# Joining the last two layers of a four-layer graph network in one loop

## The chip, the cores and the metric

The kernel runs on one core of one Trainium2 chip. The metric is device time in microseconds (us) of one execution of the whole kernel. Before the change it is 2429.77 us, the median of 3 runs from 2427.74 to 2431.06.

The core's engines are named as in the profile: PE is TensorE (matmuls; PEld is its weight load), DVE is VectorE, ACT is ScalarE, POOL is GpSimd, SP is SyncE, which here only issues transfers. SPq and ACTq are the queues in which SP and ScalarE issue DMAs.

## The reference

A graph of 4096 nodes with 128 features each, X (4096 x 128), goes through four layers. Each layer adds its output to X and normalises every row: X = layernorm(X + layer(X, adj)). adj is a symmetric 0/1 matrix of 4096 x 4096 with ones on the diagonal. The layers are, by the numbers used in the code:

- layer 0: a hyperbolic graph convolution with sigmoid attention
- layer 1: a graph transformer with four heads
- layer 2: relu((D (adj + I) D X) W2), with D the diagonal matrix of (row sum + 1)^-0.5
- layer 3: attention with H = X W3^T + b, s = H a_s, r = H a_r, weights softmax over j, where adj is 1, of leaky_relu(s_i + r_j), and output att H

In layer 3 the softmax is computed factored. With adj of zeros and ones, exp(leaky_relu(s + r)) is exp of the larger of (s + r) and 0.2 (s + r). Divided by a factor that depends on i alone, it becomes max(exp(0.8 s_i), exp(-0.8 r_j)) exp(r_j). So one vector `rho` = exp(0.8 s), laid along the free axis, one column `col[:, 0]` = exp(-0.8 r) and features F = X exp(r) are enough: the inner loop takes one maximum and one product with adj for each element.

## The kernel before, in words

X stays in on-chip memory for the whole kernel, as 32 tiles of 128 rows. Layer 0 writes a transposed copy of adj to memory (`adjT`), cut into 8 x 8 blocks of 512 x 512 (1 MB each in float32); layers 1, 2 and 3 read it block by block. I counts output blocks of 512 nodes (four tiles of X), J the blocks that are summed over. All matmuls are in float32 and appear in the profile as two records each.

**End of layer 0.** For each of the 32 tiles, L494 adds the layer's output to X. After every fourth, `normalise_tile` (L164) is called: statistics of the four tiles on DVE (L146, L147), variance plus epsilon (L170), Sqrt on ScalarE (L171), a reciprocal on DVE (L172), and then the normalisation. Here it is called with `on_scalar=True`: DVE makes `ms` = -mean / std (L175) and ScalarE applies it (L181). Layer 1 then begins with transposes of X (L112) and, for each block of 512 columns, products pk and pq (L825, L836), whose results ScalarE and DVE split and stack.

**Layer 2** (`layer2`, L1179). With `d` = (deg + 1)^-0.5 (L1191 to L1193), Y = X d. For each I, PE sums Y^T over the eight blocks into `pa` (L1200 adds the identity, L1212 the blocks, four matmuls of 128 x 512 each). The blocks are fetched into eight buffers `at` (L1210), even J from ScalarE's queue, odd J from SP's. DVE checks each block for values other than 0 and 1 (`odd`, L1222). After the eighth block ScalarE copies `pa` (L1227), PE multiplies with W2 into `pb` (L1230), DVE scales and clips (L1234), adds to X (L1236), and `normalise_tile(I)` follows, on DVE at L185.

**Layer 3** (`layer3`, L1240). It starts when layer 2 has ended. Small matrices are prepared from W3 and the attention vectors: `us`, `ur`, `cb`, `wx` (L1259 to L1285). X is transposed as a whole (L1289), `pr` (L1292) gives r for each tile, `psr` (L1299) gives s along the free axis, DVE adds the bias to give `rho` (L1300) and takes maxima of the absolute values (L1301). The column sums of X (`pm`, L1307) go to `tot`. A maximum over all of these and over `odd` is compared with LIMIT; all engines read the flag `fi` (L1321) and branch: `attend_factored` if the values are small and adj is plain, else `attend`, a general version that this input does not take.

`attend_factored` (L1327) first makes the exps (L1335 to L1339), F = X exp(r) (L1341, L1342) and X + bias (L1344), and then loops over I and J. A block is fetched into six buffers (L1350). For each of its four slices, DVE makes w = max(rho, col) x adj (L1354, four buffers) and PE multiplies it with F into `pa` (L1357). After the last block ScalarE copies `pa`, PE multiplies with `wx` into `pb` (L1367), DVE divides and adds to X (L1372), `normalise_tile(I)` follows and the rows go out (L1376).

**What sets the order.** Apart from the loop of layer 1, no order is written by hand: a scheduler places each engine's instructions by dependences and its own estimates, so an instruction can stand earlier or later on its engine than in the source. Every engine, and each queue that issues DMAs, works through its instructions in that order. ScalarE's activation functions come in table sets; where a function of a set that is not loaded stands next, the build puts a table load (ACT_TABLE_LOAD) before it.

Of the kernel before, what the change touches and what calls it, by code (L numbers as in the profile page):

```python
# [9 lines left out]
F32 = mybir.dt.float32  # L10
# [6 lines left out]
P = 128  # L17
# [13 lines left out]
class Net:  # L31
# [132 lines left out]
    def normalise_tile(self, I, on_scalar=False):  # L164
# [6 lines left out]
        nc.scalar.activation(rs, rs, AF.Sqrt)  # L171
        nc.vector.reciprocal(rs, rs)  # L172
# [1006 lines left out]
    def layer2(self, weight):  # L1179
        nc, tc, N, NT, NS, D, X = self.nc, self.tc, self.N, self.NT, self.NS, self.D, self.X  # L1180
        with ExitStack() as ctx:
            keep = ctx.enter_context(tc.tile_pool(name="keep2", bufs=1))
            rot = ctx.enter_context(tc.tile_pool(name="rot2", bufs=2))
            at2 = ctx.enter_context(tc.tile_pool(name="at2", bufs=8))
            ps_a = ctx.enter_context(tc.tile_pool(name="ps_a", bufs=2, space=PSUM))
            ps_b = ctx.enter_context(tc.tile_pool(name="ps_b", bufs=2, space=PSUM))
            Y = keep.tile([P, NT, D], F32, tag="Y", name="Y")
            w = self.load_mat(weight, "w2")

            d = self.deg  # L1190
            nc.vector.tensor_scalar(d, d, 1.0, 1e-8, op0=ALU.add, op1=ALU.add)  # L1191
            nc.scalar.activation(d, d, AF.Sqrt)
            nc.vector.reciprocal(d, d)  # L1193
            for t in range(NT):
                nc.vector.tensor_scalar(Y[:, t, :], X[:, t, :], d[:, t : t + 1], None, op0=ALU.mult)
            for I in range(NS):

                pa = ps_a.tile([P, S], F32, tag="pa", name="pa")
                for b in range(4):
                    nc.tensor.matmul(  # L1200
                        pa[:, b * P : (b + 1) * P],
                        lhsT=Y[:, 4 * I + b, :],
                        rhs=self.ident,
                        start=(b == 0),
                        stop=False,
                        skip_group_check=True,
                    )
                for J in range(NS):
                    at = at2.tile([P, 4, S], F32, tag="at", name="at")
# [19 lines left out]
                for b in range(4):  # L1229
                    nc.tensor.matmul(pb[:, b, :], lhsT=a[:, b * P : (b + 1) * P], rhs=w, start=True, stop=True)  # L1230
# [251 lines left out]
```

## Time and profile before

| what | value |
|---|---|
| median of the runs | 2429.77 us (2427.74 to 2431.06, 3 runs) |
| the profiled execution | 2428.91 us, span 2427.1 us |
| busy share of the span: PE, DVE, ACT, POOL | 84%, 79%, 61%, 3% |
| mean granted clock of PE | 0.919 |
| chain that ended last: PE, DVE, ACT, issue, DMA | 58%, 24%, 12%, 3%, 2% |
| L1357, matmuls of layer 3: 512, two records each | 9% of the chain on the page |
| L1212, matmuls of layer 2: 512 records | 223.1 us busy, no idle time before them |

The profile is of one execution. Its times count from the start of the span. Each line of a timeline has start, length, engine, line, operation, tile written <- tiles read, shapes, how many were merged, and in brackets how long the engine was idle before and what it waited for. "x2 records" of a float32 matmul are one instruction. Layer 0 ends near 977 us, layer 2 begins near 1884, layer 3 near 2130. The shares are averages over stages with different limits, so the stages concerned are read one by one.

### The profile page before, as it was taken

How to read it: one execution, taken by the hardware profiler on the slowest of the kernel's cores; microseconds unless marked ns; L12 is line 12 of the kernel's file. 1: busy time of each engine (PE TensorE's matmuls, PEld its weight loads, DVE VectorE, ACT ScalarE, POOL GpSimd, SP SyncE). 2: the span in 40 equal slices, each digit the busy share in tenths (PEclk: the TensorE clock that was granted, in tenths of full speed). 3: DMA queues.
4: the chain of work that ended last, by engine and by line, in shares of the span. 5: the costliest groups of instructions: out<-in, count | busy, mean ns of one | idle time of the engine just before them, and what ended most of it. 6: DMA issues, size and time to landing. Idle time of an engine off the chain costs nothing.

```text
span 2427.1 us, 24381 instructions
## 1 busy us (share of the span) xinstructions
PE 2048.1 (84%) x8923; PEld 1138.3 (47%) x8923; DVE 1910.2 (79%) x2726; ACT 1486.0 (61%) x1793; POOL 69.5 (3%) x87
## 2 busy tenths in 40 slices
PE   4477887787777771889999999999998899979998
PEld 4266666566666650634333333433333344444443
DVE  6478888788778888767877878777787887668887
ACT  5688889888888877478777787878776000010000
POOL 2000000000000051100000000000000000000000
PEclk7689989899888885999999999999999899979999
DMA  2455466555555630154454444545444788528774
GB/s 52 139 185 200 143 207 210 172 181 183 186 169 173 195 105 1 61 200 171 154 182 153 168 173 154 176 158 179 158 160 162 279 287 284 206 104 298 286 286 170
DMA packets 103768, 431.44 MB, mean 178 GB/s; under 512 B 8976, under 2 KB 19280, under 8 KB 62672
## 3 DMA queue, kind: packets, MB, share of 16 engines
q1 hardware_dynamic: 85200, 295.50, 35.9%
q10 hardware_dynamic: 18432, 134.23, 15.9%
q8 instruction: 74, 1.21, 0.2%
q14 instruction: 62, 0.51, 0.1%
HBM read 356.26 MB, written 73.43 MB: 177 GB/s over the span
## 4 chain that ended last, share of the span: by engine, by line
PE 58%; DVE 24%; ACT 12%; issue 3%; DMA 2%; SPq 0%; ACTq 0%; POOL 0%; DVEq 0%; POOLq 0%
PE pv L965 15%; PE pa L1357 9%; PE pa L1212 9%; PE ps L939 9%; DVE e L948 5%; PE pz L583 4%; DVE w L606 3%; PE pi L674 3%; DVE w L636 3%; DVE t L632 3%; PE ptA L564 3%; ACT t L628 3%; ACT e L946 2%; ACT at L572 2%; ACT w L601 1%
## 5 line engine op out<-in xcount | busy, mean ns | idle before, releaser
L948 DVE SCALAR_TENSOR_TENSOR e<-at,e 128x2048 f32<-128x2048 f32 x256 | 581.6, 2287 | 181.0 <-ACT e L946 171.3
L946 ACT ACTIVATE e<-ps 128x1024 f32<-128x1024 f32 x512 | 489.4, 1025 | 130.6 <-PE ps L939 101.8
L965 PE MATMUL pv<-e,VA 128*64 128x512 f32 x2048 | 503.5, 613 | 12.2 <-DVE e L948 12.2
L939 PE MATMUL ps<-QS,KS 128*128 128x512 f32 x1024 | 313.1, 425 | 27.7 <-ACT e L946 23.3
L939 PEld LDWEIGHTS ps<-QS,KS 128*128 128x128 f32 x1024 | 173.3, 190 | 246.0 <-ACT e L946 153.6
L674 PE MATMUL pi<-HA,w 128*128 128x129 f32 x1152 | 186.7, 337 | 83.2 <-DVE w L636 83.2
L965 PEld LDWEIGHTS pv<-e,VA 128*64 128x64 f32 x2048 | 126.0, 137 | 258.1 <-issue 232.2
L1357 PE MATMUL pa<-w,F 128*128 128x512 f32 x512 | 223.2, 597 | 12.2 <-DVE w L1354 12.2
L674 PEld LDWEIGHTS pi<-HA,w 128*128 128x128 f32 x1152 | 179.8, 249 | 93.8 <-DVE w L636 93.8
L1212 PE MATMUL pa<-at,Y 128*128 128x512 f32 x512 | 223.1, 596 | 0.0
L1354 DVE SCALAR_TENSOR_TENSOR w<-rho,col,at 128x512 f32<-128x512 f32 x256 | 186.7, 746 | 18.9 <-PE pa L1357 1.7
L591 DVE SCALAR_TENSOR_TENSOR t<-ei,de,pz 128x512 f32<-128x512 f32 x144 | 107.2, 747 | 106.5 <-PE pz L583 102.7
L564 PE MATMUL ptA<-ident,ad 128*128 128x128 f32 x1032 | 146.0, 287 | 42.9 <-ACT at L572 35.7
L1222 DVE SCALAR_TENSOR_TENSOR odd<-at 128x2048 f32<-128x2048 f32 x64 | 146.6, 2290 | 38.3 <-DMA at<-adjT 37.6
L564 PEld LDWEIGHTS ptA<-ident,ad 128*128 128x128 f32 x1032 | 124.9, 148 | 99.4 <-ACT at L572 53.3
L572 ACT COPY at<-ptA 128x512 f32<-128x512 f32 x200 | 108.3, 587 | 99.0 <-PE ptA L564 98.8
L583 PE MATMUL pz<-HT 128*128 128x512 f32 x292 | 161.6, 664 | 4.9 <-DVE w L655 4.5
L1357 PEld LDWEIGHTS pa<-w,F 128*128 128x128 f32 x512 | 97.3, 192 | 133.9 <-issue 100.1
L1212 PEld LDWEIGHTS pa<-at,Y 128*128 128x128 f32 x512 | 97.5, 192 | 120.0 <-issue 118.8
L606 DVE TENSOR_TENSOR w<-w,at 128x2048 f32<-128x2048 f32 x64 | 143.7, 2281 | 0.0
L1361 ACT COPY a<-pa 128x512 f32<-128x512 f32 x8 | 4.7, 586 | 206.1 <-PE pa L1357 206.1
L931 ACT ACTIVATE nat<-nat 128x2048 f32<-128x2048 f32 x64 | 122.7, 1918 | 1.9 <-DMA nat<-in_adj_dram 1.9
(351 smaller groups left out, 2448.8 us busy)
## 6 DMA issues: line engine op xcount, KB each, us to landing
at<-adjT SPq DMA_DIRECT2D x128, 1024.0 KB, 4.8
ad<-in_adj_dram SPq DMA_DIRECT2D x64, 1024.0 KB, 6.5
adjT<-at SPq DMA_DIRECT2D x64, 1024.0 KB, 8.3
nat<-in_adj_dram ACTq DMA_DIRECT2D x64, 1024.0 KB, 4.9
at<-adjT ACTq DMA_DIRECT2D x64, 1024.0 KB, 4.8
dj<-rows SPq DMA_DIRECT2D x28, 256.0 KB, 7.6
X<-in_x_dram SPq DMA_DIRECT2D x4, 512.0 KB, 6.5
di<-rows SPq DMA_DIRECT2D x8, 256.0 KB, 8.4
```

Of the source, the lines that this page charges most:

```text
L564: nc.tensor.transpose(pt[:, ib, :], st[p]["ad"][k][:, ib, jb * P : (jb + 1) * P], self.ident)
L572: copy(st[p]["at"][k][:, jb, :], st[p]["pt"].pop(m))
L583: nc.tensor.matmul(pz, lhsT=HT[:, j * P : (j + 1) * P], rhs=HT[:, I * S : (I + 1) * S], start=True, stop=True)
L606: nc.vector.tensor_tensor(w, w, at, ALU.mult)
L674: nc.tensor.matmul(self.po[ib // 2][:, ib % 2, :], lhsT=w[0][:, jb, ib * P : (ib + 1) * P], rhs=HA[:, 4 * J + jb, :], start=False, stop=(J ...
L939: nc.tensor.matmul(p[:, h, :], lhsT=KS[:, h2 + h, jb * P : (jb + 1) * P], rhs=QS[I % 2][:, h2 + h, :], start=True, stop=True,)
L946: nc.scalar.activation(e[:, h2 : h2 + 2, :], p, AF.Exp)
L948: nc.vector.scalar_tensor_tensor(e, at[:, jb % 4, :].unsqueeze(1).to_broadcast([P, NH, S]), 0.0, e, op0=ALU.not_equal, op1=ALU.mult,)
L965: nc.tensor.matmul(st["po"][h // 2][g : g + 64, :], lhsT=VA[:, o : o + 64], rhs=e[:, h, :], start=(jb == 0), stop=(jb == NT - 1), skip_gro ...
L1212: nc.tensor.matmul(pa, lhsT=Y[:, 4 * J + jb, :], rhs=at[:, jb, :], start=False, stop=(J == NS - 1 and jb == 3), skip_group_check=True,)
L1354: nc.vector.scalar_tensor_tensor(w, rho[:, I * S : (I + 1) * S], col[:, 0, j : j + 1], at[:, jb, :], op0=ALU.max, op1=ALU.mult)
L1357: nc.tensor.matmul(pa, lhsT=F[:, j, :], rhs=w, start=False, stop=(j == NT - 1), skip_group_check=True)
```

## The change

- `normalise_tile` makes 1/std with two ScalarE activations, Ln and then Exp with scale -0.5, where it had Sqrt on ScalarE and a reciprocal on DVE. It is called at the end of layer 0 and for every I of layers 2 and 3.
- `layer2` and `layer3` become one function, `layers23`. The small matrices of layer 3 are made before layer 2's loop. The rest of layer 3's preparation becomes `prepare(I)`, called after `normalise_tile(I)`: transposes of the four tiles, `pr`, `psr`, bias and clamping of r and s to 40 in size, maxima, the three exps, F, and X + bias, which has a buffer of its own, `XB`.
- The column sums of X come from ScalarE's copy of the transposed tiles (an accumulated sum, `part`), and one transpose at the end, in place of the `pm` matmuls.
- The `at` buffers of layer 2 become six instead of eight. Three buffers `ahead` hold the blocks (0, 0) to (0, 2) for layer 3; their fetches are written after the flag and before the branch, and `attend_factored` reads them instead of fetching these blocks again.
- `attend`, the general version, takes over buffers and is no longer pipelined.

```diff
@@ normalise_tile
-        nc.scalar.activation(rs, rs, AF.Sqrt)
-        nc.vector.reciprocal(rs, rs)
+        nc.scalar.activation(rs, rs, AF.Ln)
+        nc.scalar.activation(rs, rs, AF.Exp, scale=-0.5)
@@ layers23 (was layer2, layer3)
+            ahead = [keep.tile([P, 4, S], F32, tag=f"ahead{J}", name=f"ahead{J}") for J in range(3)]
             F = keep.tile([P, NT, D], F32, tag="F", name="F")
+            XB = keep.tile([P, NT, D], F32, tag="XB", name="XB")
...
-            at2 = ctx.enter_context(tc.tile_pool(name="at2", bufs=8))
+                atp = pctx.enter_context(tc.tile_pool(name="at2", bufs=6))
...
+                def prepare(I):
+
+                    s, tl = slice(I * S, (I + 1) * S), slice(4 * I, 4 * I + 4)
+                    p = self.ps_t.tile([P, 4, P], F32, tag="pt", name="pt")
+                    for b in range(4):
+                        nc.tensor.transpose(p[:, b, :], X[:, 4 * I + b, :], self.ident)
+                    XT = rot.tile([P, S], F32, tag="XT", name="XT")
+                    nc.scalar.activation(
+                        XT, p.rearrange("p a b -> p (a b)"), AF.Identity, accum_out=part[:, I : I + 1]
+                    )
+                    pr = ps_s.tile([P, S], F32, tag="ps", name="pr")
+                    for b in range(4):
+                        nc.tensor.matmul(
+                            pr[:, b : b + 1], lhsT=XT[:, b * P : (b + 1) * P], rhs=ur, start=True, stop=True
+                        )
+                    ps = ps_s.tile([P, S], F32, tag="ps", name="psr")
+                    nc.tensor.matmul(ps, lhsT=us, rhs=XT, start=True, stop=True)
+                    r = rot.tile([P, 4], F32, tag="r", name="r")
+
+                    nc.vector.tensor_scalar(r, pr[:, 0:4], cb[:, 1:2], 2.0 * LIMIT, op0=ALU.add, op1=ALU.min)
+                    nc.vector.tensor_scalar(r, r, -2.0 * LIMIT, None, op0=ALU.max)
+                    nc.scalar.activation(col[:, 0, tl], r, AF.Exp, scale=-0.8)
+                    nc.scalar.activation(col[:, 1, tl], r, AF.Exp)
+                    nc.vector.tensor_reduce(mx[:, I : I + 1], r, AX.X, ALU.max, apply_absolute_value=True)
+                    nc.vector.tensor_scalar(rho[:, s], ps, cb[:, 0:1], 2.0 * LIMIT, op0=ALU.add, op1=ALU.min)
+                    nc.vector.tensor_reduce(
+                        mx[:, NS + I : NS + I + 1], rho[:, s], AX.X, ALU.max, apply_absolute_value=True
+                    )
+                    nc.scalar.activation(rho[:, s], rho[:, s], AF.Exp, scale=0.8)
+                    for t in range(4 * I, 4 * I + 4):
+                        nc.vector.tensor_scalar(
+                            F[:, t, 0 : D - 1], X[:, t, 0 : D - 1], col[:, 1, t : t + 1], None, op0=ALU.mult
+                        )
+                    nc.vector.tensor_copy(F[:, tl, D - 1], col[:, 1, tl])
+                    nc.vector.tensor_tensor(
+                        XB[:, tl, :], X[:, tl, :], br.unsqueeze(1).to_broadcast([P, 4, D]), ALU.add
+                    )
...
-                self.normalise_tile(I)
+                    self.normalise_tile(I)
+                    prepare(I)
+
+                nc.vector.tensor_reduce(part[:, NS : NS + 1], part[:, 0:NS], AX.X, ALU.add)
+                p = self.ps_t.tile([P, 4, P], F32, tag="pt", name="pm")
+                nc.tensor.transpose(p[0:1, 0, :], part[:, NS : NS + 1], self.ident)
+                nc.scalar.copy(tot[:, 0 : D - 1], p[0:1, 0, 0 : D - 1])
...
                 nc.vector.tensor_scalar(fi, ma[0:1, :], LIMIT, None, op0=ALU.is_le)
+                for J, at in enumerate(ahead):
+                    (nc.sync if J % 2 else nc.scalar).dma_start(out=at, in_=self.adjT[0, J])
@@ attend_factored
-            nc.scalar.activation(col[:, 0, :], col[:, 1, :], AF.Exp, scale=-0.8)
-            nc.scalar.activation(col[:, 1, :], col[:, 1, :], AF.Exp)
-            for c in range(NS):
-                s = slice(c * S, (c + 1) * S)
-                nc.scalar.activation(rho[:, s], rho[:, s], AF.Exp, scale=0.8)
-            for t in range(NT):
-                nc.vector.tensor_scalar(F[:, t, 0 : D - 1], X[:, t, 0 : D - 1], col[:, 1, t : t + 1], None, op0=ALU.mult)
-            nc.vector.tensor_copy(F[:, :, D - 1], col[:, 1, :])
-            for t in range(NT):
-                nc.vector.tensor_tensor(X[:, t, :], X[:, t, :], br, ALU.add)
...
-                    at = at3.tile([P, 4, S], F32, tag="at", name="at")
-                    (nc.sync if J % 2 else nc.scalar).dma_start(out=at, in_=self.adjT[I, J])
+                    if I == 0 and J < len(ahead):
+                        at = ahead[J]
+                    else:
+                        at = at3.tile([P, 4, S], F32, tag="at", name="at")
+                        (nc.sync if J % 2 else nc.scalar).dma_start(out=at, in_=self.adjT[I, J])
...
-                            X[:, t, :], pb[:, b, 0:D], rd[:, k : k + 1], X[:, t, :], op0=ALU.mult, op1=ALU.add
+                            X[:, t, :], pb[:, b, 0:D], rd[:, k : k + 1], XB[:, t, :], op0=ALU.mult, op1=ALU.add
```

In the changed kernel the fetches of layer 2 are L1300, its matmuls L1302, the transposes, `pr` and `psr` of `prepare` L1253, L1260 and L1264, the fetches of `ahead` L1346, the products of layer 3 L1374 (w) and L1377, and L1364 stands for L1347.

## The prediction

> **What bounds the kernel now.** I read the chain of waits first, then the timeline where the change touches it. From the last aggregation of layer 2 to the first of layer 3 the chain leaves the large matmuls (columns: start, us, engine, line):
>
> ```profile
> 2102.75 27.48 PE pa L1212 x64
> ...
> 2130.95 1.17 PE pb L1230 x8
> ...
> 2157.40 6.03 PE pm L1307 x54
> ...
> 2166.59 12.25 DMA at<-adjT
> ...
> 2179.62 1.49 DVE X L1344 x7
> ...
> 2181.82 30.66 PE pa L1357 x66
> ```
>
> The gap runs from 2130.23 to 2181.82: 51.6 us of preparation, branch, exps and F/X products. On both sides TensorE is full. This table of one layer-2 tile and one layer-3 tile (window, length, PE, PEld, DVE, ACT busy) shows it:
>
> ```profile
> 1985.32:2014.68 29.36, 29.36 (x82) 14.02 (x81) 22.29 (x36) 0.79 (x2) 0.00 (x0) 1.00 0.82 285
> 2242.20:2271.81 29.61, 29.61 (x76) 13.23 (x75) 26.53 (x53) 0.79 (x2) 0.00 (x0) 1.00 0.81 293
> ```
>
> So TensorE work that moves into the layer-2 loop is paid there. The edit of `normalise_tile` reaches a third place, the end of layer 0, where ScalarE chains the eight tiles into layer 1 (timeline):
>
> ```profile
> 952.34 1.28 ACT L171 ACT_TABLE_LOAD   x1
> ...
> 956.54 0.20 ACT L171 ACTIVATE rs<-rs 128x4 f32<-128x4 f32 x1 [2.92 <-DVE rs L170]
> ...
> 958.75 1.65 ACT L181 ACTIVATE X<-X,ms,rs 128x128 f32<-128x128 f32 x4 [2.01 <-DVE ms L175]
> ...
> 975.61 1.65 ACT L181 ACTIVATE X<-X,ms,rs 128x128 f32<-128x128 f32 x4 [1.27 <-DVE ms L175]
> ...
> 978.37 0.69 ACT L828 ACTIVATE hi<-pk,bkc 128x512 fp32r<-128x512 f32 x1 [1.12 <-PE pk L825]
> ```
>
> One table load serves all eight Sqrts. Last, the start of layer 2 (timeline):
>
> ```profile
> 1871.77 2.58 SPq L1210 DMA_DIRECT2D at<-adjT  x4
> ...
> 1881.98 1.11 DVE L1028 TENSOR_SCALAR X<-X,mv,rs 128x128 f32<-128x128 f32 x4 [0.51 <-ACT rs L1024]
> ...
> 1887.16 2.06 ACTq L1210 DMA_DIRECT2D at<-adjT  x4
> ...
> 1891.97 2.29 DVE L1222 SCALAR_TENSOR_TENSOR odd<-at 128x2048 f32<-128x2048 f32 x1 [3.59 <-DMA at<-adjT]
> ...
> 1895.11 1.92 PE L1212 MATMUL pa<-at,Y 128*128 128x512 f32 x2
> ```
>
> SP fetches its four tiles while layer 1 still ends; ScalarE's queue issues J=0 at 1887.16, it lands 4.8 us later, and PE starts at 1895.1.
>
> **What the Trainium skill says.** "ScalarE: Activation LUTs", section "What ACT_TABLE_LOAD costs": 1283 ns for a load plus some 1380 ns of drain. The trace has the 1.28, but no drain: a load at 949.26 is followed by its activation at 950.55. I use 1.28. The same page, "Table sets: the hidden batching unit": Ln and Exp share one set, so one load could do; but the changed program's instruction order has a load before every Ln and another before every Exp of `normalise_tile` (two different sets), also in layer 0. "DMA: Bandwidth & Descriptors", section "Issuing engines are not separate DMA queues": SP's and ScalarE's transfers run on the same 16 engines and interleave. The trace agrees: J=0 alone takes 4.8 us to land, four together a median of 8.2.
>
> **The change part by part** (against the profiled execution's 2428.9 us, span 2427.1; the median 2429.8 lies 0.9 above it).
>
> 1. *End of layer 0: +18.2.* Per tile ScalarE now does load 1.28, Ln 0.20, load 1.28, Exp 0.20, with gaps 3.02 us, where it did 0.20. From the first Ln at 956.54: 8 x 3.02 less the first load (hidden as before) = 22.9; 8 x L181 at 1.65 = 13.2; three XT copies at 0.59 = 1.8; about 1.0 of waits for ms. That is 38.9, so L181 ends at 995.4 instead of 977.3. The PE order is unchanged: pk L825 stands behind the first transpose of the last tile, L828 behind pk and behind L181 on ScalarE, and everything of layer 1 behind these. No cover: ScalarE was the chain already. All of it passes through. Ends: 17 and 19.5.
>
> 2. *Start of layer 2: +4.7.* The three `ahead` fetches stand last in the source, but they wait for nothing, and in the built order they stand before the first `at` fetches: ahead1 on SP, ahead0 and ahead2 on ScalarE's queue. And SP's first `at` now waits for the last DVE result of layer 1 (L1028, 1883.1), since its buffer lies elsewhere; before it went at 1871.8. So from 1883.2 SP fetches J=1,3,5 and from 1887.16 ScalarE's queue ahead0, ahead2, J=0: 6 MB flow before J=0 is complete. At 0.42 MB/us (the DMA view of this stretch has 411 to 439 GB/s) and 2 us to begin, that is 1885.2 + 14.5 = 1899.7, against a PE start at 1895.1. DVE does us/ur/cb/wx (some 2 us) and all 32 Y (0.2 each) until 1896.2, so it is not last. Ends: +1.2 (only Y binds) and +6.
>
> 3. *Layer-2 loop, matmuls: +16.8.* Each tile adds four transposes (0.59 in the chain), four pr (0.82) and psr (0.97): 2.4 us on the full engine; seven tiles fall in the loop. Ends: 15 and 19.
>
> 4. *Layer-2 loop, waits: +9.1.* PE's order puts the transposes ten matmuls after pb: 1.89 + 10 x 0.858 = 10.5 us after the tile's last matmul (T). What they wait for: with six `at` buffers, J=4 of the next tile is issued at T-3.4 and lands at T+1.4; DVE's order has its odd check (2.33) ahead of o, so o is T+3.8 to 4.9; odd of J=5 (lands T+4.9) to 7.3; X 0.7, statistics 1.15, rs 0.15: 9.3; Ln 0.2, load 1.28, Exp 0.2: 11.1; four normalisations of 0.28 to 12.2; last transpose 12.4 instead of 11.1. So 1.3 us stall a tile, seven times; behind the waiting transposes stand all further matmuls. DVE itself is not full: 22.3 + 3.7 (two r operations 0.3, two mx 0.85, rho 0.75, F 0.9, XB 0.7, less a reciprocal) in 33 us. Ends: 0 (landing or DVE 1.3 us earlier) and 15.
>
> 5. *Gap: -35.3.* From T: copy 0.65, pb to 1.9, o to 3.0, X to 3.75, statistics and rs to 5.1, Ln 5.3 (its load hidden), load and Exp to 6.8, normalise to 8.0, transposes 8.2, XT with its sum 9.0, pr 10.0, r twice 10.4, exps 10.9, F four times 11.8, rho 12.6, its maximum 13.25, then maximum, transpose, fi as before (0.9) 14.2, branch 0.75: 15.0; w 0.75, and L1364 on a PE with a low clock (0.52 granted in 2165 to 2182; there L1347 twice took 3.75): PE's first product at about 16.3 instead of 51.6. The first tiles lie ready; J=3 is issued at 15, lands by 22, needed at 26. Ends of the new gap: 15 and 20.
>
> 6. *Layer 3, seven tile ends: +2.1.* DVE's normalisation waits for Ln, load, Exp (1.75 from rs) instead of Sqrt and reciprocal (0.5), with only one w between. w has four buffers, 3.4 us of lead; before, at the tile end of 2271.65, the ninth w came at 2278.3 and PE needed it at 2271.65 + 8 x 0.858 = 2278.5. The added 1.3 is mostly met by the 1.05 of L1347, which now stands after nine of the next tile's products instead of at its beginning. I take 0.3 each; ends 0 and 1.
>
> 7. *End: +1.3.* The same chain after the last product: Ln, load, Exp for these two:
>
> ```profile
> 2421.95 0.21 ACT L171 ACTIVATE rs<-rs 128x4 f32<-128x4 f32 x1 [3.57 <-DVE rs L170]
> 2422.19 0.18 DVE L172 RECIPROCAL rs<-rs 128x4 f32<-128x4 f32 x1 [0.27 <-ACT rs L171]
> ```
>
> The XB buffer, the clamping of r and the fallback branch (not taken) cost nothing on the path: they are DVE time in a loop with 7 us of slack, or not executed; without that slack XB would be 0.7 a tile.
>
> Sum: 18.2 + 4.7 + 16.8 + 9.1 - 35.3 + 2.1 + 1.3 = +16.9, so 2445.8 for the profiled execution and **2446.7** for the median.
>
> **Rivals.** (a) *Likeliest, as above*, 2440 to 2453: chance 0.60. (b) *The in-order waits bite harder*: 2 us a tile in layer 2 (+5), 1 us at each layer-3 tile end (+5), a gap of 20 (+4): 2461. For it: ScalarE holds queue, loads and `at` issues in one order; against it: six buffers are 20 us of lead. 0.17. (c) *The joined work is hidden*: no stall in the loop (-9.1), start bound by Y alone (-3.5): 2434. For it: a DMA often lands faster; against it: the loop's chain has four links of over 1 us. 0.14, a third of it inside 0.2%. (d) *The other side: the loads cost nothing*, because a set already resident is not loaded again. Then part 1 is 0, part 4 is 0, parts 6 and 7 are 0, the gap 1.3 shorter: 4.7 + 16.8 - 36.6 = -15.1: 2414.7. It decides (faster by 0.2%, 4.9 us) below 0.4 us a load, by proportion between +16.9 at 1.28 and -15.1 at 0. Against it: every load in this trace takes 1.28. 0.05. (e) *The fetch ahead doesn't do what it says*: it is issued at the wrong end, as part 2 has it; without its harm (b to d aside) 2442, inside (a). 0.04.
>
> **Numbers.** 2446.7; the range 2435 to 2459 reaches into (b) and (c) and leaves out (d) and the far ends. About 0.2% is what a measurement of this kernel can tell from no change. Faster by more: 0.05 (d); within: 0.06 (a third of c, a little of a); slower: 0.89. The likeliest case's own range is 2440 to 2453.
>
> **What would show it.** Right: 16 loads between the last X L494 and L828, and L828 44 us after the Tanh at L488 instead of 26; PE's first L1302 about 18 us after DVE's L1028 (before: 13); tiles of 33 us in layer 2 with a wait of some 1 us at L1253 for DVE; 16 us between the last L1302 and the first L1377; tiles of 29.6 to 30 in layer 3. Wrong: tiles of 31.8 or less (no stall), loads absent or shorter, L1302 starting with Y, or layer-3 tiles above 30.5.

## The result, and the profile after

The changed kernel takes 2459.48 us (median of four runs, 2451.25 to 2459.8), the kernel before 2429.53 (four runs beside them): a ratio of 1.0115, 95% interval 1.0093 to 1.0138. The prediction was 2446.7, slower, with a range of 2435 to 2459: the sign is right, the size is 13 us short. The median lies half a microsecond above the range; as a ratio (2459 to 2429.77 is 1.0120) the measured 1.0115 is just inside it. The profiled execution took 2459.8 us, its span is 2457.9; that of before was 2427.1. The difference of the spans, 30.8 us, divides so (each stretch from the same two marks in both timelines; the marks are named in the table, that of L1028 is the start of its last four):

| stretch | before | after | difference | predicted |
|---|---|---|---|---|
| up to the Tanh of L488 (no edit reaches it) | 952.1 | 957.1 | +5.0 | 0 |
| Tanh to the first L828, end of layer 0 | 26.28 | 43.92 | +17.6 | +18.2 |
| first L828 to the last L1028, layer 1 | 903.6 | 904.2 | +0.6 | 0 |
| L1028 to the first aggregation matmul of layer 2 | 13.13 | 20.59 | +7.5 | +4.7 |
| first to last aggregation matmul of layer 2 | 235.1 | 262.2 | +27.1 | +25.9 |
| gap to the first product of layer 3 | 51.6 | 18.6 | -33.0 | -35.3 |
| first to last product of layer 3 | 235.9 | 240.6 | +4.7 | +2.1 |
| end | 9.4 | 10.8 | +1.4 | +1.3 |

The chain of waits of the changed kernel over the gap (start, us, engine, line), which answers to the first fence of the prediction. Here and below x counts records: two for each float32 matmul, one for each transpose, so that the 512 records of L1357 or L1377 are 256 matmuls.

```profile
2169.98 18.04 PE pa L1302 x42
...
2193.45 1.28 ACT L172
...
2197.41 1.87 PE pr L1260 x8
2199.27 1.93 PE psr L1264 x2
...
2204.62 2.04 PE pa L1364 x2
2206.66 30.08 PE pa L1377 x64
```

The exps, the F products and the first transfers are gone from the chain. What is left is one tile's normalisation and preparation, with a table load in it, and three pieces of TensorE work that take twice their usual time: the four pr took 0.97 us and psr 0.97 in the tile before, and L1364 takes 1.05 ahead of the next tile.

One layer-2 tile and one layer-3 tile (window, length, PE, PEld, DVE, ACT busy, POOL, granted clock, DMA share, GB/s):

```profile
2022.46:2055.77 33.31, 32.34 (x96) 15.59 (x95) 25.32 (x46) 5.19 (x10) 0.00 (x0) 1.00 0.71 252
2269.54:2299.43 29.89, 29.77 (x77) 13.18 (x76) 26.56 (x52) 3.56 (x6) 0.00 (x0) 1.00 0.79 290
```

TensorE is no longer busy all the time in layer 2. The timeline of that tile shows where it stands (the bracket is the idle time ahead of the group and what ended it):

```profile
2022.46 8.75 PE L1302 MATMUL pa<-at,Y 128*128 128x512 f32 x20
2032.18 1.10 PE L1253 MATMUL pt<-ident,X 128*128 128x128 f32 x4 [0.97 <-DVE X L185]
2033.11 1.02 PE L1302 MATMUL pa<-at,Y 128*128 128x512 f32 x2
2034.05 1.05 PE L1260 MATMUL pr<-ur,XT 128*128 128x1 f32 x8
2034.97 1.11 PE L1264 MATMUL psr<-XT,us 128*128 128x512 f32 x2
```

The transposes wait for the normalised X and are then paced by its four pieces, which DVE ends 0.26 us apart (0.93 us from the first transpose to the next matmul). Six tiles have such a wait; it lasts 0.96 to 1.34 us, 1.13 in the mean.

The end of layer 0 on ScalarE's timeline: the single load has become sixteen between the Tanh and L828. Only the first lies in time in which ScalarE waits anyway (2.92 us, for rs).

```profile
957.35 1.28 ACT L171 ACT_TABLE_LOAD   x1
961.55 0.21 ACT L171 ACTIVATE rs<-rs 128x4 f32<-128x4 f32 x1 [2.92 <-DVE rs L170]
961.77 1.28 ACT L172 ACT_TABLE_LOAD   x1
...
963.69 1.65 ACT L181 ACTIVATE X<-X,ms,rs 128x128 f32<-128x128 f32 x4 [0.42 <-DVE ms L175]
965.36 1.28 ACT L171 ACT_TABLE_LOAD   x1
...
1001.02 0.69 ACT L828 ACTIVATE hi<-pk,bkc 128x512 fp32r<-128x512 f32 x1 [1.12 <-PE pk L825]
```

And the start of layer 2 (timeline, all engines). The fetches ahead stand in front of J=0 on both queues, and SP's first three `at` go only after L1028; TensorE waits 10.3 us for J=0:

```profile
1897.26 0.33 SPq L1346 DMA_DIRECT2D ahead<-adjT  x1
...
1905.18 1.11 DVE L1028 TENSOR_SCALAR X<-X,mv,rs 128x128 f32<-128x128 f32 x4 [0.51 <-ACT rs L1024]
1906.50 1.28 SPq L1300 DMA_DIRECT2D at<-adjT  x3
...
1908.36 0.83 ACTq L1346 DMA_DIRECT2D ahead<-adjT  x2
...
1925.77 4.61 PE L1302 MATMUL pa<-at,Y 128*128 128x512 f32 x5 [10.28 <-DMA at<-adjT]
```

I don't count the first row of the table to the change: in the eleven profiled executions of this study, none of which differs in an edit ahead of that point, the Tanh starts between 950.8 and 957.5 us. The execution of before (952.1) was drawn from the lower half and that of after (957.1) from the upper end. A joined kernel can be as early as before: that without any load has its Tanh at 952.0, after the same TensorE, VectorE and ScalarE instructions. The time of the kernel before alone ranges from 2424.76 to 2439.32 us over its runs. The changes in the other rows are therefore read by stretch, and not from totals of single executions.

### The profile page after: what moved, and what is told of

Read it like the earlier page. It is cut to its first block, busy times and chain, and to the rows that moved or that the text cites. A ratio compares the mean times of both kernels' runs of the same rounds, so it can differ in the third digit from the quotient of the medians.

```text
span 2457.9 us, 24298 instructions
## 1 busy us (share of the span) xinstructions
PE 2051.9 (83%) x8860; PEld 1134.0 (46%) x8860; DVE 1908.5 (78%) x2698; ACT 1557.6 (63%) x1893; POOL 69.8 (3%) x87
## 3 DMA queue, kind: packets, MB, share of 16 engines
q1 hardware_dynamic: 85200, 295.50, 35.3%
## 4 chain that ended last, share of the span: by engine, by line
PE 53%; DVE 26%; ACT 14%; issue 3%; DMA 3%; ACTq 0%; SPq 0%; POOL 0%; DVEq 0%; POOLq 0%
PE pv L965 14%; PE ps L939 9%; PE pa L1377 7%; PE pa L1302 7%; DVE e L948 5%; PE pz L583 4%; DVE w L606 3%; PE pi L674 3%; DVE w L636 3%; PE ptA L564 3%; DVE t L632 3%; ACT t L628 3%; DMA at<-adjT 2%; ACT e L946 2%; ACT at L572 2%
## 5 line engine op out<-in xcount | busy, mean ns | idle before, releaser
L1302 PE MATMUL pa<-at,Y 128*128 128x512 f32 x512 | 226.4, 599 | 10.3 <-DMA at<-adjT 10.3
L1377 PE MATMUL pa<-w,F 128*128 128x512 f32 x512 | 225.7, 599 | 2.0 <-DVE w L1374 1.4
L1374 DVE SCALAR_TENSOR_TENSOR w<-rho,col,at 128x512 f32<-128x512 f32 x244 | 178.3, 748 | 18.5 <-PE pa L1377 1.4
L1302 PEld LDWEIGHTS pa<-at,Y 128*128 128x128 f32 x512 | 97.5, 193 | 127.4 <-issue 126.7
L1377 PEld LDWEIGHTS pa<-w,F 128*128 128x128 f32 x512 | 96.9, 192 | 126.3 <-issue 100.2
L642 PE MATMUL ptz<-ident,t 128*128 128x128 f32 x448 | 68.7, 294 | 67.5 <-DVE w L655 45.6
```

What stands on the lines that cost most here:

```text
L1302: nc.tensor.matmul(pa, lhsT=Y[:, 4 * J + jb, :], rhs=at[:, jb, :], start=False, stop=(J == NS - 1 and jb == 3), skip_group_check=True,)
L1374: nc.vector.scalar_tensor_tensor(w, rho[:, I * S : (I + 1) * S], col[:, 0, j : j + 1], at[:, jb, :], op0=ALU.max, op1=ALU.mult)
L1377: nc.tensor.matmul(pa, lhsT=F[:, j, :], rhs=w, start=False, stop=(j == NT - 1), skip_group_check=True)
```

## The experiments

My theory is the prediction's sum: table loads on ScalarE's chain, the fetches ahead in front of layer 2's first tiles, and in the joined loop the added matmuls and a wait of the transposes. The rivals are named in each expectation. The stretches of all profiled executions, in us, with the ratio of the timed runs to the kernel before, which ran beside each (the names are those of the headings below):

| kernel | end of layer 0 | start of layer 2 | its loop | gap | layer 3 | end | ratio |
|---|---|---|---|---|---|---|---|
| before | 26.3 | 13.1 | 235.1 | 51.6 | 235.9 | 9.4 | 1 |
| after | 43.9 | 20.6 | 262.2 | 18.6 | 240.6 | 10.8 | 1.0115 |
| Ln and Exp alone | 43.9 | 11.5 | 234.0 | 55.0 | 238.7 | 10.8 | 1.0083 |
| no loads in layer 0 | 25.0 | 20.5 | 262.2 | 18.6 | 240.5 | 10.8 | 1.0016 |
| fetches with the last tile | 43.9 | 14.2 | 266.7 | 18.6 | 240.5 | 10.7 | 1.0096 |
| fetches behind the last copy | 43.9 | 14.4 | 264.6 | 18.6 | 239.7 | 10.8 | 1.0060 |
| joined work later | 43.9 | 20.4 | 249.2 | 18.6 | 241.0 | 10.7 | 1.0061 |
| no loads at all | 25.0 | 20.3 | 254.8 | 17.3 | 237.2 | 9.4 | 0.9954 |
| all together | 25.0 | 14.4 | 249.7 | 17.3 | 237.7 | 9.4 | 0.9920 |
| with eight fill matmuls | 25.0 | 14.1 | 249.9 | 16.8 | 238.1 | 9.4 | 0.9910 |
| with fitted fill | 25.0 | 14.4 | 249.6 | 15.0 | 235.7 | 9.5 | 0.9897 |

### One part alone: Ln and Exp in the kernel before

In the kernel before, only these lines of normalise_tile:

```diff
-        nc.scalar.activation(rs, rs, AF.Sqrt)
-        nc.vector.reciprocal(rs, rs)
+        nc.scalar.activation(rs, rs, AF.Ln)
+        nc.scalar.activation(rs, rs, AF.Exp, scale=-0.5)
```

> The kernel before with one part of the change alone: in normalise_tile, Ln and Exp in place of Sqrt and reciprocal; layers 2 and 3 stay apart. My theory (the table loads are the loss, wherever the chain passes ScalarE): the stretch from the Tanh of L488 to the first L828 grows from 26.3 to 44 us as in the joined kernel (+17.6); nothing in the layer-2 loop; the gap between the two aggregations about +1.4 (one load and one more activation behind the last rs); the seven tile ends of layer 3 from 0 to +4.6 in all; the end +1.35. Sum +20 to +25: 2450 to 2454 us. Rival A (the loss at the end of layer 0 comes with the joined build's other buffers and orders, and not with the loads): 26 to 30 us there, 2430 to 2437 in all. Rival B (the longer layer-3 tiles of the joined kernel, +4.6, come from its other work and not from the loads): layer 3 from first product to last end stays at 235.9 and the sum is at most +20.5; if they come from the loads, it reads about 240.

Measured: 2449.37 us (2444.84 to 2458.58), ratio to before 1.0083 (1.0057 to 1.0108). Tanh to L828 43.94, as in the joined kernel; gap 55.0 (+3.4); layer 3 238.7 (+2.8), its tiles 29.88 instead of 29.61; end 10.75 (+1.3). Rival A falls. The edit of these lines alone, without any joining, costs some 70% of the whole loss (0.0083 of 0.0115; the interval leaves half to nine tenths). Rival B is half right: of the +4.7 of layer 3, 2.8 come with the loads, and 1.9 do not (part 6 below has them). The gap grew by 2 us more than I expected, and the start of layer 2 was 1.6 shorter; neither was followed up. In the chain of waits of a layer-3 tile end of this kernel, the load is the 1.24 us that the chain calls issue, between the two activations:

```profile
2262.99 0.21 ACT rs L171
2263.21 0.06 ACT L172
2263.27 1.24 issue
2264.51 0.21 ACT rs L172
```

### The loads of layer 0 taken away, the activations kept

```diff
             nc.vector.tensor_tensor(gf, gf, self.to_ball("gp2", th), ALU.mult)
+            self.tc.keep_in_program_order(nc.scalar.preload_act_table_set("natural_log_exp_and_others"))
```

> The changed kernel, with one addition ahead of the end of layer 0: the table set that holds both Ln and Exp is loaded there once, by name, behind the Tanh. Of the 16 loads between the Tanh and L828 one is left; the 16 Ln and Exp stay. My theory (each load is paid in full on ScalarE's chain): the stretch from the Tanh to L828 falls from 43.9 to 27 to 29 us, and the time by 15 to 17: about 2443. Rival A (it is the handover of two activations and ms between DVE and ScalarE that is paid, and the loads run in the shadow of DVE's statistics): the stretch stays above 38 and the time above 2453. Rival B (what is gained is lost again, since layer 1 behind it is bound otherwise): L828 comes earlier, but the span from L828 to layer 2's start grows by as much, and the time stays within 3 us of 2459.

Measured: 2434.36 us (19 runs, 2433.07 to 2439.0), ratio to before 1.0016 (1.0008 to 1.0025). Tanh to L828 24.98, which is 1.3 shorter than with Sqrt: Ln and Exp follow each other on ScalarE and the reciprocal's trip to DVE is gone, so that the first L181 waits 0.23 us for ms and not 2.01. Layer 1 did not grow (902.9). The timeline of ScalarE:

```profile
956.49 1.28 ACT L492 ACT_TABLE_LOAD   x1
960.69 0.20 ACT L171 ACTIVATE rs<-rs 128x4 f32<-128x4 f32 x1 [2.92 <-DVE rs L170]
960.93 0.21 ACT L172 ACTIVATE rs<-rs 128x4 f32<-128x4 f32 x1
961.36 1.65 ACT L181 ACTIVATE X<-X,ms,rs 128x128 f32<-128x128 f32 x4 [0.23 <-DVE ms L175]
```

The fifteen loads were 15 x 1.28 = 19.2 us of chain, and 18.9 came back by stretch. The total fell by 25 against the changed kernel, which did not run beside it; the stretches of layers 2 and 3 are equal to 0.1 us, so the stretch at the end of layer 0 is what counts. The spans of the two profiled executions differ by 21.3, of which 0.9 lies ahead of the Tanh and 1.3 in layer 1; the rest of the 25 is not placed.

### The fetches ahead at another place

First behind the last `at` fetches of layer 2:

```diff
+                    for J, at in enumerate(ahead if I == NS - 1 else ()):
+                        tc.keep_in_program_order((nc.sync if J % 2 else nc.scalar).dma_start(out=at, in_=self.adjT[0, J]))
                     a = rot.tile([P, S], F32, tag="a", name="a")
                     nc.scalar.copy(a, pa)
...
-                for J, at in enumerate(ahead):
-                    (nc.sync if J % 2 else nc.scalar).dma_start(out=at, in_=self.adjT[0, J])
```

> The changed kernel with the three fetches ahead moved: they are issued behind the adj fetches of layer 2's last tile on the same queues (J=6 on ScalarE's, J=7 on SP's), and no longer ahead of layer 2's first fetches. Theory A (the 3 MB ahead of J=0 are what is late at layer 2's start): from DVE's L1028 to the first L1302 20.6 us falls to 13 to 14.5, where the 32 Y bind, and the time by 6 to 7.5: about 2452.5. Theory B (it is SP's wait for L1028 ahead of its first three fetches that is late, which this leaves as it is): the stretch stays at 17 to 20.6 and the time above 2456. At the other end both expect the gap between the aggregations unchanged at 18 to 19 us, since nothing else is fetched there; if the late fetches hold up layer 2's last tile or J=3 of layer 3, the gap and the first tile of layer 3 grow by 2 to 5 us.

Measured: 2453.15 us (2451.9 to 2456.41), ratio 1.0096 (1.0077 to 1.0115). The start of layer 2 is 14.16: theory A, with 1.0 us left over before's 13.13, in which SP's wait for L1028 remains. The timeline at that point:

```profile
1902.06 1.28 SPq L1300 DMA_DIRECT2D at<-adjT  x3
...
1904.19 0.34 ACTq L1300 DMA_DIRECT2D at<-adjT  x1
...
1914.88 2.90 PE L1302 MATMUL pa<-at,Y 128*128 128x512 f32 x3 [3.83 <-issue]
```

J=0 now lands 10.5 us after its issue instead of 15.9: three tiles of SP's are under way, but not the fetches ahead. The gap kept its 18.58. But the last tile of layer 2 took 38.8 us instead of 33.3: the three fetches share the engines with the adj fetches whose odd checks stand ahead of X on DVE (the landing in that tile's chain takes 8.45 us instead of 4.80). TensorE's timeline shows a long wait, although in this build the transposes of that tile stand behind 17 matmuls and not 10, and then work at half speed:

```profile
2162.61 0.84 PE L1253 MATMUL pt<-ident,X 128*128 128x128 f32 x3 [3.47 <-DVE X L185]
...
2166.27 1.71 PE L1260 MATMUL pr<-ur,XT 128*128 128x1 f32 x8
2167.84 2.05 PE L1264 MATMUL psr<-XT,us 128*128 128x512 f32 x2
```

So they were put behind the copy of the last tile, where layer 2 fetches nothing more (the old place is emptied as above):

```diff
                     nc.scalar.copy(a, pa)
+                    for J, at in enumerate(ahead if I == NS - 1 else ()):
+                        tc.keep_in_program_order(nc.scalar.dma_start(out=at, in_=self.adjT[0, J]))
```

> The changed kernel with the three fetches ahead behind the copy of the last tile's product (L1317), all on ScalarE's queue, so that they run while layer 2 fetches nothing more. In the run that put them behind the last two adj fetches, layer 2 began 6.4 us earlier (14.2 instead of 20.6 us behind L1028), but layer 2's last tile took 38.8 us instead of 33.3. Theory A (it is the 3 MB beside other fetches that costs, at either end): the start stays at 14, the last tile is back at 33.3 to 33.6, the first to last L1302 at 262; the gap stays at 18.6, since 3 MB at the 0.42 MB/us seen at full load land some 10 us behind the copy. About 2450 to 2453 us. Theory B (three transfers on one queue land too late for layer 3): the gap is 20 us or longer.

Measured: 2447.0 us (2445.24 to 2451.23), ratio 1.006 (1.0041 to 1.0079). Start 14.37, last tile 33.33, gap 18.58: theory A in all three. The loop was 264.6 and not 262, because of one tile in its middle, of 37.04 us, in the profiled execution (2451.23, the slowest of the five). No extra transfer is near it:

```profile
2088.36 1.10 PE L1253 MATMUL pt<-ident,X 128*128 128x128 f32 x4 [1.52 <-DVE X L185]
2089.30 1.73 PE L1302 MATMUL pa<-at,Y 128*128 128x512 f32 x2
2090.82 1.71 PE L1260 MATMUL pr<-ur,XT 128*128 128x1 f32 x8
```

The wait is 1.52 us here, and what follows runs at half speed again, with a granted clock of 0.50 from 2090 to 2096. In four executions with this loop (after, no loads in layer 0, and the two of this section) 22 waits of the transposes of 0.94 to 1.40 us were followed by work at full speed; the two of 1.52 and 3.47 were not. In the chain of this tile 0.40 us lie between adj's landing and the odd check on DVE, where the changed kernel has 0.04; where they come from stays open.

### The joined work later in the next tile

```diff
                         for jb in range(4):
...
+                        if J in (3, 4) and I:
+                            step(I - 1, J - 3)
...
                     self.normalise_tile(I)
-                    prepare(I)
+                step(NS - 1, 0, False)
+                step(NS - 1, 1, False)
```

`step(I, 0)` holds the transposes and XT of `prepare`, `step(I, 1)` all the rest; the transposes and pr are kept in program order behind the aggregation's matmuls of J = 3 and J = 4. In the tile of the changed kernel shown above they stand behind 10 and 11 matmuls.

> The changed kernel with the joined work of a tile put later in the next tile's matmuls: the four transposes stand behind 16 of them (10 to 11 before), pr and psr behind 20 (13 before). The number of instructions is the same. In the changed kernel's tile from 2020.62 PE waits 0.97 us before the transposes for DVE's X of L185, and the added matmuls take some 2.9 us (transposes, pr and psr, with what they break in the row of L1302); the tile is 33.4 us where it was 29.4. My theory: the wait goes and the matmuls stay: a tile of 32.2 to 32.6, the loop from first L1302 to last end 255 to 256.5 instead of 262.3, the time about 2453. Rival A (all of the 4 us is TensorE's own work; a wait taken away at one place comes back at pr, psr or a later L1302): the tile stays at 33 to 33.5 and the time within 2 us of 2459. Rival B (DVE is the bound of the joined loop: later r, rho and F push the odd checks and with them the fetches): the tile grows above 33.5, and the time above 2460.

Measured: 2445.11 us (2444.85 to 2445.7), ratio 1.0061 (1.0043 to 1.0078). Tiles of 31.49, the loop 249.2: below my figure. The gap is unchanged (18.59). TensorE's timeline of one tile:

```profile
1999.42 0.60 PE L1256 MATMUL pt<-ident,X 128*128 128x128 f32 x4
1999.86 3.60 PE L1307 MATMUL pa<-at,Y 128*128 128x512 f32 x8
2003.29 0.95 PE L1265 MATMUL pr<-ur,XT 128*128 128x1 f32 x8
2004.10 1.10 PE L1269 MATMUL psr<-XT,us 128*128 128x512 f32 x2
2005.05 10.46 PE L1307 MATMUL pa<-at,Y 128*128 128x512 f32 x24
```

From start to start the transposes take 0.44, pr 0.81, psr 0.95: 2.2 us, and a tile grows by 2.13 over before's 29.36. Both rivals fall. The 1.9 us a tile between this and the changed kernel is waiting: 1.13 is the mean of the brackets, 0.49 more is the transposes paced by L185's four pieces (0.93 instead of 0.44), and some 0.2 lies at pr and at the matmul ahead of it.

### No table load in any normalise_tile

The addition in layer 0 as above, this one in layer 2, and the same set once more at the head of attend_factored:

```diff
-                nc.scalar.activation(d, d, AF.Sqrt)
+                nc.scalar.activation(d, d, AF.Sqrt); tc.keep_in_program_order(nc.scalar.preload_act_table_set("natural_log_exp_and_others"))
```

> The changed kernel with the set of Ln and Exp loaded by name once ahead of the end of layer 0, once in layer 2 behind the Sqrt of the degrees, and once at the head of layer 3: no load is left before any Ln or Exp of normalise_tile. My theory: the end of layer 0 takes 25 us as in the run with the first of these alone; the transposes of layer 2 wait 1.28 us less, so a tile goes from 33.4 to 32.1 and the loop from 262 to about 253; the gap loses 1.3 (17.3), layer 3's seven tile ends lose 0.28 each (29.6 a tile, 238.5 from first product to last end), the end loses 1.2 (9.5). About 2421 us, 13 below the run with the first load alone. Rival A (the transposes wait for DVE's odd check and adj's landing, and a faster rs only moves the wait): the tile stays at 33 or more and the time at 2428 to 2432. Rival B (layer 3's longer tile ends are not the loads): 29.88 a tile stays.

Measured: 2421.62 us (2418.33 to 2422.83), ratio 0.9954 (0.9939 to 0.9968): faster than before. Tiles of 32.0 to 32.4, the loop 254.8, gap 17.34, layer 3 237.2 with tiles of 29.69, end 9.44. My theory holds, with a loop 1.8 above its figure; both rivals fall. The Trainium skill's statement that one load serves Ln and Exp ("ScalarE: Activation LUTs", "Table sets: the hidden batching unit") is true here once the set is named; left to itself, the build put one load ahead of each. It is also the prediction's rival (d), made true by other means: without the loads the change is a gain, 12 us against the 15 that (d) worked out.

### All together, and TensorE's clock

This kernel has the three loads by name, the fetches ahead behind the last copy, and the joined work later:

```diff
+                nc.scalar.activation(d, d, AF.Sqrt); tc.keep_in_program_order(nc.scalar.preload_act_table_set("natural_log_exp_and_others"))
...
+                        if J in (3, 4) and I:
+                            step(I - 1, J - 3)
...
+                        tc.keep_in_program_order(nc.scalar.dma_start(out=at, in_=self.adjT[0, J]))
```

> All together: the joined kernel with the three loads by name, the fetches ahead behind the last tile's copy, and a tile's transposes 16 and pr and psr 20 matmuls into the next tile. If the causes are apart and add up: end of layer 0 25.0, start of layer 2 14.2, tiles of 31.5 and a loop of 249 to 250, gap 17.2, layer 3 238.5, end 9.5. With some 954 us ahead of the Tanh and 903 in layer 1 that is a span of 2411 and a time of about 2412: some 18 us below the kernel before. Rival (the same wait was counted twice: once the transposes stand later, the loads were hidden in the loop anyway, and layer 2's fetches now bind): the loop stays at 252 or more, and the time is 2416 or more.

Measured: 2413.2 us (2409.69 to 2415.65), ratio 0.992 (0.9902 to 0.9938). End of layer 0 24.98, start 14.41, loop 249.7, gap 17.32, layer 3 237.7, end 9.44: each within 1 us of the expectation. The rival of double counting falls as to the sum; it is true in the loop, where the later transposes alone gave 249.2, so that the loads inside the loop are then hidden.

Next, eight matmuls that nobody reads, to find out whether the low clock in the gap is a cause or a trait of the place (`fill(n)` issues n matmuls of 128x512):

```diff
+                fill(7)
                 step(NS - 1, 0)
                 step(NS - 1, 1)
+                fill(1)
```

> The kernel with all together, and eight matmuls of 128x512 added whose result nobody reads: seven behind the last tile's pb, where TensorE waits some 6 us for DVE, and one behind psr. In the changed kernel the clock granted to TensorE is 0.50 from 2195 to 2210, which covers pr, psr, L1364 and the first products of layer 3. Theory A (the grant falls because TensorE idles, and comes back some 5 us after it is busy): the clock is 0.8 or more by pr and psr; pr, psr and L1364 take 1.0 each instead of 1.9 to 2.0, the gap falls by 2 to 3 us and layer 3's first tile by 2; 4 us below the kernel with all together. Theory B (the low grant belongs to what ran before, and comes back at its own time): the clock stays at 0.50, the fill itself takes 1.7 us each, the transposes wait for it, and the time is 3 to 8 us above.

Measured: 2410.21 us (2409.57 to 2412.69), ratio 0.991 (0.9893 to 0.9927). Theory A for the first half: pr took 1.05 and psr 1.10 as groups instead of 1.87 and 2.05, at a clock of 1.00. But seven were too many (the transposes came 7.0 us behind pb instead of 5.4), and two waits of 1.31 and 1.20 us around pf brought the clock down again, so that L1379, the first matmul of layer 3, took 2.04 for its two passes as before. The gap gained 0.5. Hence the fill fitted to the waits, with one matmul more behind pm and one behind pf:

```diff
-                fill(7)
+                fill(5)
...
+                tc.keep_in_program_order(nc.tensor.transpose(p[0:1, 0, :], part[:, NS : NS + 1], self.ident)); fill(1)
...
+                tc.keep_in_program_order(nc.tensor.transpose(p[0:1, 0, :], ma, self.ident)); fill(1)
```

> As the run with eight idle matmuls, with the fill fitted to the waits: five (not seven) behind the last pb, one behind psr, one behind pm and one behind pf. In the run with eight, the clock stayed at 1.00 up to psr, but the transposes came 1.6 us later than without fill, and after two waits of 1.3 and 1.2 us around pf the first product of L1379 and the first tile of layer 3 were slow again (2.04 us for two; clock 0.57 to 0.74). Theory A (a wait of some 1.2 us or more, on top of another shortly before, brings the clock down; short waits do not): now L1379 takes 1.1 instead of 2.04, layer 3's first tile 28.7 instead of 30.7 from first product to its pb, the gap 15 to 15.5 instead of 17.3: some 4 us below the kernel without fill, 2408 to 2410. Theory B (the branch into layer 3 itself brings the clock down): L1379 stays at 2.04 and the first tile at 30.5 or more, and the gap alone gains 1.5.

Measured: 2410.2 us (2406.14 to 2411.77), ratio 0.9897 (0.988 to 0.9913). The gap is 15.03 (17.32 without fill), layer 3 235.7 (237.7), its first tile 28.72 (30.73): theory A in each figure. The total gained less than the 4 expected of it against the kernel without fill (2413.2, ratios 0.9897 and 0.992, whose intervals overlap), and its median is that of the run with eight fills (2410.21); in the profiled execution the Tanh was at 957.45, the latest of all. The gain of the fill is thus shown by the stretches alone. The kernel without fill, then that with it (window of five us over L1373 or L1379 and the first products; the eighth figure is the granted clock):

```profile
2160.00:2165.00 5.00, 3.21 (x4) 1.07 (x5) 3.56 (x8) 1.91 (x2) 0.00 (x0) 0.50 0.35 93
```

```profile
2160.00:2165.00 5.00, 3.95 (x11) 1.22 (x9) 3.81 (x11) 2.17 (x3) 0.00 (x0) 1.00 0.15 21
```

This is the version that beats both kernels: about 1.0% below before, and 2.2% below the changed kernel by the two ratios (0.9897 / 1.0115).

## Why the prediction was right, and where its terms were off

**Part 1, end of layer 0 (+18.2; measured +17.6).** Right in mechanism and size: sixteen loads, none covered but the first, everything behind them. The run that keeps the activations and takes the loads away shows it (43.9 to 25.0).

**Part 2, start of layer 2 (+4.7; measured +7.5, above the end of 6 that I gave).** The mechanism is right, one term of the sum is mis-sized: "6 MB flow before J=0 is complete". J=0 landed 15.9 us after its issue at 1909.51. From two us after SP's first issue (1908.5) to then, at 0.42 MB/us, some 7.1 MB passed. The six blocks themselves are 6.3 MB (1024 KB each), and ScalarE's queue had J=2 and J=4 in flight too, which share the engines with J=0. That last share is worked out, not measured apart. Moving the fetches took 6.2 to 6.4 us off; about 1 us is left, in which SP's wait for L1028 still stands. That wait was not tried alone. The Trainium skill's statement that SP's and ScalarE's transfers interleave on the same engines ("DMA: Bandwidth & Descriptors", "Issuing engines are not separate DMA queues") holds here to its full price: J=0 took 4.8 us to land with nothing ahead of it, 10.5 with SP's three under way, and 15.9 with two fetches ahead in front of it on its own queue as well. The four fetches that the prediction gives as agreement are all of one queue and do not show it.

**Parts 3 and 4, the loop of layer 2 (+16.8 and +9.1; measured together +27.1).** The sum is right within 1.2 us, but by two errors that nearly cancel, which is luck: with the transposes later, 14.1 are left for the matmuls (2.7 less than I gave), and 13.0 were waiting (3.9 more). In part 3 I took the four transposes at 0.59 and pr and psr at 0.82 and 0.97; where nothing waits they take 0.44, 0.81 and 0.95, and a tile grows by 2.13 instead of 2.4. In part 4 the step "last transpose 12.4 instead of 11.1" is nearly right: in the tile shown the transposes end 1.46 late (0.97 of waiting and 0.49 of pacing), in the mean of the six 1.62. What it left out is what stands behind them: pr comes just one matmul after the transposes, starts 0.15 us behind the end of its XT copy, and costs some 0.2 more. The links were the right ones: landing 4.80, odd check 2.30 and load 1.28 stand in the chain of the tiles. The kernel without loads bears out the division: its transposes wait for 0.06 us at most, but are still paced, and its tiles are 32.0 to 32.4, above the 31.49.

**Part 5, the gap (-35.3; measured -33.0).** The chain is as I listed it; the term that is off is the speed of TensorE: I gave it a low clock for L1364 alone, but pr and psr run at half speed too (1.87 and 1.93 instead of 0.97 each). With the clock kept up the gap is 2.3 us shorter.

**Part 6, layer 3 (+2.1; measured +4.7).** The longer tile ends are there, and the term for them is a little small: with the loads alone the stretch grows by 2.8, with 29.88 instead of 29.61 from one tile's start to the next. What I missed has nothing to do with the loads. In the kernel before, two L1347 stand ahead of the first product, in the gap. In the changed kernel one L1364 stands there, and that of the second tile follows the first tile's products (timelines of before and after):

```profile
2165.82 3.75 PE L1347 MATMUL pa<-eps,tot 1*128 1x512 f32 x4 [1.19 <-DVE fi L1319]
```

```profile
2236.67 1.12 PE L1364 MATMUL pa<-eps,tot 1*128 1x512 f32 x2
```

This piece, 1.05 us in the chain, has moved from the gap into layer 3. The clock adds to it: behind the first product it stays at 0.50 for 4.90 us, in the run with Ln and Exp alone for 3.62, and half of the difference, 0.64, is lost. Together that is 1.7 of the 1.9 us that do not come with the loads (a sum worked out from the timelines, not a run). A low clock at the start of layer 3 is not new, however: in the kernel before it lasts 4.18 us (before, then after):

```profile
2181.82:2186.00 4.18, 4.18 (x5) 1.84 (x6) 3.04 (x5) 0.00 (x0) 0.00 (x0) 0.50 0.34 102
```

```profile
2206.59:2211.49 4.90, 4.90 (x7) 2.19 (x7) 2.14 (x3) 0.00 (x0) 0.00 (x0) 0.50 1.01 425
```

The 2.0 us that the fill takes off layer 3 are therefore a gain over both kernels, and not the missing term.

**Part 7 (+1.3; measured +1.4).** Right.

**What was not in the sum.** The 5.0 us ahead of the Tanh, which no edit reaches. Without them the spans differ by 25.8, against 16.9 in the sum; of these 8.9 us, the start has 2.8, the loop 1.2, the gap 2.3, layer 3 2.6.

**The rivals.** Rival (b), at 2461, has the measured time and not the reasons: its stall of 2 us a tile is close (1.9), but a tile end of layer 3 costs 0.4 (2.8 over seven) and not 1, the matmuls are cheaper than in my sum, and 5.0 of the measured difference are those ahead of the Tanh. Rival (c) is excluded: nothing joined was hidden as it stood; the stall goes only with the work placed later, and the matmuls stay even then. Rival (d) failed on its premise, since each load takes 1.28 us, and was shown right in its consequence. Rival (e) is part 2: a fetch ahead that is ready from the start is issued at the start.

## What to carry to other kernels

A table load of 1.28 us is small until it stands between two engines in a chain that repeats: count loads by the built order of instructions and not by the functions in the source, and name one set that holds all of a stage's functions. Work moved into a loop whose bound is an in-order engine should stand there only where its operands are long ready; here six matmuls later were worth 13 us of 27. And a transfer that waits for nothing went out first here, whatever its line: give it a place in its queue at which the engines of the DMA are free.

## What the runs showed of the hardware that I had not expected

TensorE's clock falls after short waits. Waits of 0.94 to 1.40 us left it at 1.00, one of 1.52 brought it to 0.50 for 6.8 us, and 1.31 followed by 1.20 with one transpose between did so too (0.57 in the next five us). But the length of a single wait is not the measure. In each of the eleven traces all changes of the granted clock lie whole multiples of 3.41 us apart, so I cut the traces at these points and counted TensorE's idle time in every stretch of 3.41 us that ran at 1.00 (the ends of matmuls in the profile are modelled, so the limits are rough):

| idle in the stretch | stretches | the next one at 0.50 |
|---|---|---|
| below 1.4 us | 5743 | 6 |
| 1.4 to 2.0 us | 322 | 99 |
| 2.0 us or more | 427 | 427 |

So it is the sum within one such stretch that counts, and from 2.0 us on the clock always fell. The wait of 1.52 was an early case. The two waits of 1.31 and 1.20 fall in one stretch and leave TensorE busy for 0.98 us of it. And busy is not the whole measure either: two of the six early falls, in the kernel before and in that with Ln and Exp alone, come behind a stretch with no idle time at all, filled with the one-column pr and with psr. Why it fell there stays open. The three stretches (the wait of 1.52, the two waits with eight fills, the kernel before):

```profile
2086.07:2089.48 3.41, 1.89 (x7) 0.76 (x6) 1.62 (x6) 1.69 (x3) 0.00 (x0) 1.00 0.87 308
```

```profile
2157.32:2160.73 3.41, 0.98 (x4) 0.16 (x2) 2.30 (x9) 1.03 (x3) 0.00 (x0) 1.00 0.00 0
```

```profile
2145.05:2148.47 3.42, 3.42 (x26) 2.82 (x24) 0.75 (x1) 0.00 (x0) 0.00 (x0) 1.00 0.00 0
```

The Trainium skill ("TensorE: Matmul & The Clock Gate", "What's actually happening") has the two speeds and a free-running window of some 3.4 us, and the steps of 3.41 agree; its advice to avoid idle gaps over about 3 us ("Why this matters for your kernels") is too generous for this kernel, where 2 us of idle time in one stretch were always enough. The changed kernel's loop had at most 1.26 us of idle time in one stretch. In the two executions in which the clock fell in this loop, the tile concerned took 3.6 and 5.4 us more, the longer waits included. That useless matmuls in a wait can shorten a kernel by 4 us of its stretches was the other surprise.
